# A fused attention and feed-forward block on one core: sums over eight chunks by a second transfer, both halves of the maxima on DVE, and rotary halves swapped by transfers

## The chip, the cores and the metric

The kernel runs on one core of a Trainium2 chip. The core has five engines with their own instruction streams: PE (TensorE, matrix products), DVE (VectorE), ACT (ScalarE), POOL (GpSimd) and SP (SyncE, which here only issues transfers). Each engine works through its own stream in order. Transfers (DMA) are issued from the queues of SP, ACT and POOL and share 16 DMA engines. The metric is the device time of one execution in microseconds, and its median over several runs.

## The reference

The input is x of shape (2, 2048, 512) in float32. The block computes a layer norm, attention with rotary positions and grouped keys (16 heads of width 32, 2 key groups), a residual, a second layer norm, and a product with a weight in fp8 values:

```python
x = x + attn(layernorm(x)); x = x + ffn(layernorm(x))
# attn, with h = layernorm(x)
q = (h @ wq + bq).reshape(b, s, 16, 32)
k = (h @ wk + bk).reshape(b, s, 2, 32);  v = (h @ wv + bv).reshape(b, s, 2, 32)
q = q * cos + rotate_half(q) * sin       # rotate_half: (-x2, x1) of the two halves of 16
k = k * cos + rotate_half(k) * sin
scores = einsum("bqhd,bkhd->bhqk", q * 32**-0.5, repeat(k)) * 32**-0.5
out = einsum("bhqk,bkhd->bqhd", softmax(scores), repeat(v)) @ wo + bo
# ffn: x and weight are scaled by max|.|/448, rounded to e4m3, multiplied, scaled back, bfloat16
```

## The kernel before

**Tiling.** The 4096 tokens are cut into 8 blocks (n) of 512. Four heads that share keys form a quad. A block has 4 quads, and each quad is treated in two halves of 256 queries: a *unit* (u), 64 in all. A unit goes over the 2048 keys of its batch element in 16 chunks (kc) of 128, four chunks to a *round* (r = 0 to 3).

**One unit.** The softmax needs the row maxima first. A generator, `scores_for_maxima` (L412 to L429), runs about one round ahead: for each of 64 combinations of 128 queries, a head and 512 keys PE writes a score tile `s` into one of two PSUM banks (L412), and DVE reduces it into `part` (L419). When a unit's tiles are through, DVE reduces `part` to `mx` (L426), ACT copies the rounded value to `mrow` (L427), and POOL writes the rest, mx minus the rounded value, beside it (L428). PE transposes `mrow` in the last round of the unit before (`mtp`, L439, in `gather_maxima`), and ACT copies the result to `mT` (L443).

In a round, `probabilities` lets PE subtract the maxima from T (L777, only for the first two chunks of a unit), add the scores of one chunk for four heads (L786), and ACT takes the exponential into a tile `p` of 128 x 1024 (L795). `columns` multiplies the four tiles `p` with the values (L746) and, into the other half of the same PSUM tile `avs`, tiles of sums with a matrix of ones (L757): the latter give the denominators.

**The sums.** To spare PE products with ones, tiles are first added. `add_pair` (L769) adds two tiles p on POOL into a tile `pa`. In rounds 0 to 2 this is done for both pairs, and a transfer on POOL's queue with an adding write (L836) adds the first `pa` to the second: `far_sum`, the sum over four chunks. Its product with ones follows one round later. In round 3 four tiles are multiplied: the far sum of round 2, the sum of the first pair, and the last two `p` as they are. A unit so has six products with ones: none in round 0, one each in rounds 1 and 2, four in round 3. Tiles `p` have five buffers, `pa` four.

**Filling work.** All else runs in gaps of this loop. Jobs are Python generators that yield the engine of their next step. `fill(kind)` takes a step from the first list (finishing, queue, beside) whose first job wants that engine: there are places for PE twice in a round (once in round 0) and for DVE twice at the end of a round. Jobs are: keys and values of the next batch element (`project_kv`), queries of the next block (`project_q`), the output product of the block before (`finish_block`), its second norm, and the feed-forward weight (`prepare_weight`, enqueued with block 4). The order is written out by hand inside `tc.manual_schedule()`; only the part behind the loop is ordered by the framework's scheduler.

**Rotary positions.** `rotated` (L274, L277) multiplies q or k on PE by a signed permutation matrix `rot_sb`, and DVE multiplies the result, in PSUM, by the sines into `u`. `rope` (L282, L283) lets POOL multiply q by the cosines and add u. `stack_queries` later splits q into a rounded part and a rest (L222, L223), writes both to DRAM and reads them back in the stacked layout `qst` (on SP's queue). Keys go the same way (`kS`, and `dkS`, differences to keys 256 earlier).

**Start and end.** Ahead of the loop, keys and values of the first batch element and the first two query tiles are projected; the jobs there use the same functions, with the flag `attending` off. Behind it, the fp8 stage goes over 16 half blocks: ACT scales (`v`, L872), DVE rounds with a helper tile `magic` (L210 to L216), PE transposes (L884), ACT copies (`xqT`, L886), PE multiplies (L889), ACT scales back (`y`, L893), DVE adds the residual (L894) and SP stores. `v` and `magic` take buffers of the tiles `p`.

Of the kernel before, what the change touches and what calls it, by code (L numbers as in the profile page):

```python
# [8 lines left out]
F32 = mybir.dt.float32  # L9
# [4 lines left out]
ALU = mybir.AluOpType  # L14
AX = mybir.AxisListType
# [12 lines left out]
def preln_attn_fp8_ffn_kernel(  # L28
# [60 lines left out]
    wide = ctx.enter_context(tc.tile_pool(name="wide", bufs=1))  # L89
    ppool = ctx.enter_context(tc.tile_pool(name="p", bufs=5))  # L90
    papool = ctx.enter_context(tc.tile_pool(name="pa", bufs=4))
    w2 = ctx.enter_context(tc.tile_pool(name="w2", bufs=6))
# [171 lines left out]
    def product(dst, lhs, rhs, chunks=DC):  # L264

        for c in range(chunks):
            yield ON_PE
            nc.tensor.matmul(dst, lhs(c), rhs(c), start=(c == 0), stop=(c == chunks - 1))  # L268

    def rotated(q, csb, name):  # L270

        yield ON_PE
        r = bank(f"r_{name}")
        nc.tensor.matmul(r, rot_sb, q, start=True, stop=True)  # L274
        yield ON_DVE
        u = t2(f"u_{name}")
        nc.vector.tensor_tensor(u, r, csb[:, 1, :], ALU.mult)  # L277
        return u
# [42 lines left out]
    def project_kv(n, xt, xnT, csb):  # L321
# [14 lines left out]
        nc.scalar.activation(kv, pk, AF.Identity, bias=bkv_sb)  # L336
        u = yield from rotated(kv, csb, f"k_{n}")
        yield ON_PE
        tv = bank(f"tv_{n}")
        for i in range(NT):  # L340
# [3 lines left out]
            tv.rearrange("p (i k) -> p i k", i=NT)[:, :, KD:],  # L344
        )
        rope(kx[:, BACK:], kv, u, KD, csb)
        cols = slice(blk * TB, (blk + 1) * TB)
        for what in ("kS", "dkS"):
# [9 lines left out]
            if b == 0:  # L358
                far = far.rearrange("(g d) h t -> d h g t", g=GROUPS)
                stack(  # L360
                    lambda rows: stacked[what][rows, :, cols],
                    [far[:, h, :, cols] for h in (0, 0, 1, 1)],
                )

    q_raw = {}

    def project_q(n, xnT, csb):
        q = wide.tile([P, QUADS, TB], F32, tag="q", name=f"q_{n}", bufs=2)
        for m in range(QUADS):
            pq = bank(f"pq_{n}_{m}")  # L370
            yield from product(
                pq, lambda c, m=m: wq_sb[:, c, m * P : (m + 1) * P], lambda c: xnT[:, c, :]
            )
            raw = t2(f"q_{n}_{m}")
            nc.scalar.activation(raw, pq, AF.Identity, bias=bq_sb[:, m : m + 1])
            u = yield from rotated(raw, csb, f"q_{n}_{m}")
            rope(q[:, m, :], raw, u, P, csb)
            q_raw[n, m] = q[:, m, :]

# [22 lines left out]
    def scores_for_maxima():  # L402

        for u, (k, half) in enumerate(units):
# [3 lines left out]
            for i, kb in order if u else sorted(order, key=lambda at: at[1]):  # L408
# [13 lines left out]
                if (i, kb) == (HT - 1, NKB - 1):  # L422
# [3 lines left out]
                    nc.vector.tensor_reduce(mx, part, AX.X, ALU.max)  # L426
                    nc.scalar.copy(mview[:, :, :, 0], mx)  # L427
                    nc.gpsimd.tensor_tensor(  # L428
                        mview[:, :, :, 1], mx, mview[:, :, :, 0].bitcast(F32), ALU.subtract  # L429
# [183 lines left out]
    class Job:  # L613


        def __init__(self, steps, kind=None):
            self.steps = steps
            self.kind = kind or next(steps)

        def step(self):  # L620
            self.kind = next(self.steps, None)

    queue = [Job(q0, ON_PE)]
    beside = []
    finishing = []
    attn_of = {}

    def work():

        queue[0].step()  # L630
        if queue[0].kind is None:
            queue.pop(0)

    def fill(kind, pieces=1):

        for _ in range(pieces):
            for jobs in (finishing, queue, beside):
                if jobs and jobs[0].kind in (kind, OTHER):
                    jobs[0].step()
                    if jobs[0].kind is None:  # L640
                        jobs.pop(0)
                    break

    x_res = {}
    x_taken, x_done = [], set()

# [24 lines left out]
    def enqueue(u):  # L671
        k, half = units[u]
        n, quad = quads[k]
        if half == 0 and quad == 0:
# [6 lines left out]
            if n + 1 < NBLK:  # L681
                take_x(f"q_{n + 1}")
                steps = later(project_q, n + 1, load_xnT(n + 1))
                queue.append(Job(ending(steps, f"q_{n + 1}")))
            if n == NB:
                take_x("w")
# [3 lines left out]

        first_use = (2, 0) if n <= NB else (1, 1) if n < NBLK - 1 else (0, 0)
        if n > 0 and (quad, half) == first_use:
            take_x(f"res_{n - 1}")
# [12 lines left out]
        if half == 0:  # L706
            if k + 1 < len(quads) and k + 1 not in qst:
                while quads[k + 1] not in q_raw:
                    work()
                stack_queries(k + 1)  # L710
            b = batch(k)
            if b + 1 < B and n == (b + 1) * NB - 1:
                if quad == 2:
                    fetch_keys("kS", b + 1, 0)
                    fetch_keys("dkS", b + 1, 0)
# [82 lines left out]
    with tc.manual_schedule():  # L798
        for _ in range(LEAD):
            next(scores)  # L800
        for u, (k, half) in enumerate(units):
# [9 lines left out]
            ]  # L811
            far_sum = None
            ending_soon = u >= len(units) - 2
            pieces = 2 if ending_soon else 1
            for r in range(ROUNDS):
                chunks = list(range(r * ROUND, (r + 1) * ROUND))
                last = r == ROUNDS - 1
                next(scores, None)
# [12 lines left out]
                if last:  # L831
                    sums = [far_sum, pair, *probs[2:]]
                else:
                    sums = [far_sum] if r > 0 else []
                    far_sum = add_pair(u, chunks[2], *probs[2:])
                    nc.gpsimd.dma_start(out=far_sum, in_=pair, accum_op=ALU.add)  # L836
                fill(ON_PE, pieces)
# [113 lines left out]
```

## Time and profile before

| what | value |
|---|---|
| median of 3 runs | 2548.15 us (2546.71 to 2550.91) |
| the profiled execution's own time | 2552.43 us |
| its span, first to last instruction | 2550.7 us |
| mean granted TensorE clock | 0.957 |
| busy: PE, DVE, ACT, POOL | 2308.2, 1703.0, 1209.6, 1531.0 us |
| last products of the attention loop | about 2431 us from the start |

The profile is of one execution. "Busy" is the time that an engine works on instructions; PE's is modelled and includes pipelining, so 90% is not 90% of its peak. A group of instructions is named by line, engine and operation, with the tile that it writes and those that it reads. The chain that ended last goes back from the last instruction, at each step to what released it. A list of waits puts the idle time of an engine down to the instruction that ended it: total in us, how often, the longest. The timeline gives start and duration in us, and in brackets the idle time before and what ended it; "x2" means that so many equal instructions are merged, which makes the duration that of the pair.

### The profile page before, as it was taken

Reading aid. Unit: us, or ns where it says so; the run is one execution under the profiler, and the core shown is the slowest. Engines: PE = TensorE matmul, PEld = TensorE weight load, DVE = VectorE, ACT = ScalarE, POOL = GpSimd, SP = SyncE. Lnnn points to the kernel's source line nnn. Section 1 sums busy time; section 2 is a strip of 40 time slices with the busy share of each in tenths; the row PEclk is TensorE's granted clock in tenths of the full one; section 3 lists DMA queues with packets and bytes.
Section 4 is the critical chain, followed back from the end, with each engine's and each line's share of the span. In section 5 each row is a group of like instructions: output and inputs, shape, how many; then the busy total and the mean of one; then the engine's idle time right before and its main releaser. Section 6 shows DMA issues by size and latency. Waiting matters only on the chain.

```text
span 2550.7 us, 41618 instructions
## 1 busy us (share of the span) xinstructions
PE 2308.2 (90%) x17094; PEld 1322.2 (52%) x17094; DVE 1703.0 (67%) x2706; ACT 1209.6 (47%) x1445; POOL 1531.0 (60%) x975
## 2 busy tenths in 40 slices
PE   5599999999999999988989989999989999989955
PEld 2355555555555555555555555555555555555522
DVE  3577657666677666865657786676666667667467
ACT  2155445554455444544445454445444544444545
POOL 4276756766667666665756756567656756656610
PEclk9599999999999999999999999999999999999957
DMA  7523333433234333443353433333343343343212
GB/s 227 153 50 87 79 100 83 100 92 99 60 89 91 85 100 83 109 102 64 92 121 71 92 83 67 87 72 75 67 100 91 75 116 67 72 111 100 50 42 99
DMA packets 85854, 229.77 MB, mean 90 GB/s; under 512 B 10656, under 2 KB 11296, under 8 KB 81824
## 3 DMA queue, kind: packets, MB, share of 16 engines
q0 software_dynamic: 27648, 100.68, 20.6%
q1 hardware_dynamic: 55600, 125.07, 16.3%
q8 instruction: 134, 2.20, 0.4%
q10 hardware_dynamic: 2416, 1.38, 0.2%
q14 instruction: 56, 0.46, 0.1%
HBM read 83.43 MB, written 42.99 MB: 50 GB/s over the span
## 4 chain that ended last, share of the span: by engine, by line
PE 59%; DVE 18%; POOL 7%; DMA 7%; issue 4%; ACT 4%; SPq 0%; POOLq 0%; ACTq 0%; DVEq 0%
PE s L412 15%; DVE part L419 13%; PE T L786 12%; PE avs L746 11%; PE avs L757 6%; DMA pa<-pa 6%; POOL pa L769 5%; PE po L268 4%; PE pq L268 4%; DVE both L729 2%; PE T L777 2%; ACT p L795 2%; PE py L889 2%; PE mtp L439 1%; PE r_q L274 1%
## 5 line engine op out<-in xcount | busy, mean ns | idle before, releaser
L419 DVE TENSOR_REDUCE part<-s 128x1 f32<-128x512 f32 x2048 | 1315.9, 685 | 724.8 <-PE s L412 710.9
L769 POOL TENSOR_TENSOR pa<-p,p 128x1024 f32<-128x1024 f32 x448 | 1064.6, 2381 | 566.8 <-ACT p L795 564.1
L795 ACT ACTIVATE p<-T 128x1024 f32<-128x1024 f32 x1024 | 1004.5, 1025 | 821.1 <-PE T L786 818.6
L412 PE MATMUL s<-kS,qst 128*128 128x512 f32 x2048 | 874.5, 480 | 62.3 <-DVE part L419 15.2
L786 PE MATMUL T<-qst,dkS 128*128 128x512 f32 x2048 | 682.4, 430 | 7.9 <-ACT p L795 7.9
L412 PEld LDWEIGHTS s<-kS,qst 128*128 128x128 f32 x2048 | 373.9, 192 | 500.2 <-DVE part L419 326.7
L746 PE MATMUL avs<-p,vX 128*32 128x256 f32 x8192 | 495.8, 382 | 0.0
L786 PEld LDWEIGHTS T<-qst,dkS 128*128 128x128 f32 x2048 | 374.4, 193 | 151.0 <-issue 49.9
L746 PEld LDWEIGHTS avs<-p,vX 128*32 128x32 f32 x8192 | 239.9, 110 | 216.2 <-issue 66.6
L836 POOL DMA_DIRECT2D pa<-pa x192 | 169.1, 881 | 60.7 <-POOL pa L769 57.8
L757 PE MATMUL avs<-pa,ones 128*32 128x256 f32 x2048 | 149.0, 386 | 46.7 <-DMA pa<-pa 46.7
L725 ACT COPY both<-avs 128x512 f32<-128x512 f32 x64 | 37.6, 587 | 237.2 <-PE avs L757 237.2
L268 PE MATMUL po<-wo_sb,attn 128*128 128x512 f32 x256 | 132.9, 604 | 3.4 <-POOL attn L730 3.4
L223 POOL TENSOR_TENSOR lo_q<-q,hi_q 128x512 fp32r<-128x512 f32 x32 | 41.4, 1292 | 145.9 <-ACT hi_q L222 145.8
L268 PE MATMUL pq<-xnT_q,wq_sb 128*128 128x512 f32 x224 | 118.7, 613 | 1.6 <-DVE u_q L277 1.6
L729 DVE RECIPROCAL both<-both 128x128 f32<-128x128 f32 x128 | 112.5, 920 | 5.8 <-ACT both L725 5.8
L757 PEld LDWEIGHTS avs<-pa,ones 128*32 128x32 f32 x2048 | 64.7, 110 | 96.8 <-DMA pa<-pa 56.1
L777 PEld LDWEIGHTS T<-mT,sel 128*128 128x128 f32 x512 | 79.0, 190 | 12.0 <-issue 0.4
L777 PE MATMUL T<-mT,sel 128*128 128x256 f32 x512 | 81.1, 281 | 0.0
L889 PE MATMUL py<-wT,xqT 128*128 128x512 bf16 x128 | 47.7, 513 | 29.5 <-ACT xqT L886 29.5
L730 POOL TENSOR_TENSOR attn<-both 128x256 f32<-128x256 f32 x64 | 65.6, 1024 | 7.7 <-DVE both L729 5.7
L757 PE MATMUL avs<-p,ones 128*32 128x256 f32 x1024 | 66.9, 379 | 0.0
(108 smaller groups left out, 1126.5 us busy)
## 6 DMA issues: line engine op xcount, KB each, us to landing
pa<-pa POOLq DMA_DIRECT2D x192, 512.0 KB, 4.6
qst<-q_far SPq DMA_DIRECT2D x128, 256.0 KB, 4.2
x_kv<-in_L_attn_x_dram SPq DMA_DIRECT2D x8, 1024.0 KB, 7.9
q_far<-hi_q SPq DMA_DIRECT2D x32, 256.0 KB, 2.0
q_far<-lo_q SPq DMA_DIRECT2D x32, 256.0 KB, 2.0
x_res<-in_L_attn_x_dram SPq DMA_DIRECT2D x8, 1024.0 KB, 7.5
out_dram<-v SPq DMA_DIRECT2D x16, 512.0 KB, 2.8
xnT_far<-xnT_kv SPq DMA_DIRECT2D x7, 1024.0 KB, 4.1
```

Of the source, the lines that this page charges most:

```text
L268: nc.tensor.matmul(dst, lhs(c), rhs(c), start=(c == 0), stop=(c == chunks - 1))
L412: nc.tensor.matmul(s, qst[k][:, j, at : at + P], stacked["kS"][:, group(k), kb * TB : (kb + 1) * TB], start=True, stop=True,)
L419: nc.vector.tensor_reduce(part[:, i, j, kb : kb + 1], s, AX.X, ALU.max)
L729: nc.vector.reciprocal(piece, piece)
L746: nc.tensor.matmul(avs[j * HD : (j + 1) * HD, 0, :], vX[batch(k)][:, kc, group(k), :], p[:, j, :], start=(kc == 0), stop=(kc == NTS - 1), ...
L757: nc.tensor.matmul(avs[j * HD : (j + 1) * HD, 1, :], ones, pa[:, j, :], start=False, stop=(chunks[-1] == NTS - 1 and i == len(sums) - 1), ...
L769: nc.gpsimd.tensor_tensor(pa, a, b, ALU.add)
L777: nc.tensor.matmul(T[:, j, :], sel[:, j, :], maxima[u], start=(j % 2 == 0), stop=True, skip_group_check=True,)
L786: nc.tensor.matmul(T[:, j : j + 2, :], stacked["dkS"][:, group(k), kc * P : (kc + 1) * P], qst[k][:, j : j + 2, half * HB : (half + 1) * H ...
L795: nc.scalar.activation(p, T, AF.Exp, scale=SCALE)
L836: nc.gpsimd.dma_start(out=far_sum, in_=pair, accum_op=ALU.add)
L889: nc.tensor.matmul(py, xqT[:, c, :], wT[:, c, :], start=(c == 0), stop=(c == DC - 1))
```

## The change

1. **Sums.** The far sums of rounds 0 to 2 are kept (`far_sums`) and none is multiplied before round 3. In round 2 a second adding transfer on POOL's queue adds the sum of round 0 to that of round 1, so that one tile covers eight chunks. Round 3 multiplies five tiles: the pair, two `p`, the sum over eight chunks, the far sum of round 2. Tiles `p` now have four buffers, `pa` five.
2. **Maxima.** The rounded copy into `mrow` and the subtraction both run on DVE.
3. **Rotary halves.** Inside the attention loop, `swapped` copies the halves of 16 rows crosswise into a new tile: eight transfers for a query tile, four for keys, on SP's queue. `rotate` then multiplies that tile by a sign (one value to a row) and the sines on DVE. The sign is the sum over a row of `rot_sb`, taken at the start of the kernel. This rotation and `rope` become jobs of their own (`turn`, `stack_keys`), put ahead in `beside`, and due two rounds later. Queries are written straight into the tile `q`. Ahead of the loop, `rotated` stays in use.
4. **Order.** `fill` looks at all jobs of `beside`, not only at the first, and passes over those that are not due. Loads of x for the residual are asked for when the queue is short, not at a fixed unit. `prepare_weight` is enqueued with block 6, not 4. Where queries or keys are not ready in time, `advance` steps both lists.

```diff
-    ppool = ctx.enter_context(tc.tile_pool(name="p", bufs=5))
-    papool = ctx.enter_context(tc.tile_pool(name="pa", bufs=4))
+    ppool = ctx.enter_context(tc.tile_pool(name="p", bufs=4))
+    papool = ctx.enter_context(tc.tile_pool(name="pa", bufs=5))
...
+    sign = const.tile([P, 1], F32, tag="sign", name="sign")
+    nc.vector.tensor_reduce(sign, rot_sb, AX.X, ALU.add)
+    nc.vector.tensor_scalar(sign, sign, -1.0, None, ALU.mult)
+
+    def swapped(q, rows, name):
+        t = t2(f"sw_{name}")
+        half = HD // 2
+        for at in range(0, rows, half):
+            to = at ^ half
+            nc.sync.dma_start(t[to : to + half, :], q[at : at + half, :])
+        return t
+
+    def rotate(t, csb, rows):
+        nc.vector.scalar_tensor_tensor(
+            t[:rows], t[:rows], sign[:rows], csb[:rows, 1, :], ALU.mult, ALU.mult
+        )
...
-        u = yield from rotated(kv, csb, f"k_{n}")
+        if attending[0]:
+            u = swapped(kv, KD, f"k_{n}")
+        else:
+            u = yield from rotated(kv, csb, f"k_{n}")
...
+        if attending[0]:
+            beside.insert(0, Job(stack_keys(n, kv, u, csb), due=step[0] + 2))
+        else:
+            yield from stack_keys(n, kv, u, csb)
+
+    def stack_keys(n, kv, u, csb):
+        b, blk = divmod(n, NB)
+        if attending[0]:
+            yield ON_DVE
+            rotate(u, csb, KD)
         rope(kx[:, BACK:], kv, u, KD, csb)
...
-            raw = t2(f"q_{n}_{m}")
+            raw = q[:, m, :]
             nc.scalar.activation(raw, pq, AF.Identity, bias=bq_sb[:, m : m + 1])
-            u = yield from rotated(raw, csb, f"q_{n}_{m}")
-            rope(q[:, m, :], raw, u, P, csb)
-            q_raw[n, m] = q[:, m, :]
+            if attending[0]:
+                u = swapped(raw, P, f"q_{n}_{m}")
+                beside.insert(0, Job(turn(n, m, raw, u, csb), due=step[0] + 2))
+            else:
+                u = yield from rotated(raw, csb, f"q_{n}_{m}")
+                rope(raw, raw, u, P, csb)
+                q_raw[n, m] = raw
+
+    def turn(n, m, raw, u, csb):
+        yield ON_DVE
+        rotate(u, csb, P)
+        rope(raw, raw, u, P, csb)
+        q_raw[n, m] = raw
...
-                    nc.scalar.copy(mview[:, :, :, 0], mx)
-                    nc.gpsimd.tensor_tensor(
+                    nc.vector.tensor_copy(mview[:, :, :, 0], mx)
+                    nc.vector.tensor_tensor(
                         mview[:, :, :, 1], mx, mview[:, :, :, 0].bitcast(F32), ALU.subtract
                     )
...
+            able = [
+                (jobs, job)
+                for jobs, some in ((finishing, 1), (queue, 1), (beside, len(beside)))
+                for job in jobs[:some]
+                if job.kind in (kind, OTHER) and job.due <= step[0]
+            ]
...
-            if n == NB:
+            if n == NBLK - 2:
                 take_x("w")
...
-        first_use = (2, 0) if n <= NB else (1, 1) if n < NBLK - 1 else (0, 0)
-        if n > 0 and (quad, half) == first_use:
+        soon = len(queue) <= 2 and u % (QUADS * HALVES) > 0 or n == NBLK - 1
+        if n > 0 and n - 1 not in x_asked and soon:
...
                 if last:
-                    sums = [far_sum, pair, *probs[2:]]
+                    sums = [pair, *probs[2:], *far_sums[1:]]
                 else:
-                    sums = [far_sum] if r > 0 else []
-                    far_sum = add_pair(u, chunks[2], *probs[2:])
-                    nc.gpsimd.dma_start(out=far_sum, in_=pair, accum_op=ALU.add)
+                    sums = []
+                    far_sums.append(add_pair(u, chunks[2], *probs[2:]))
+                    nc.gpsimd.dma_start(out=far_sums[r], in_=pair, accum_op=ALU.add)
+                if r == 2:
+                    nc.gpsimd.dma_start(out=far_sums[1], in_=far_sums[0], accum_op=ALU.add)
```

## The prediction

> **What bounds the kernel now.** First the page: which engine is full, and what the chain that ended last is made of.
>
> ```profile
> PE 2308.2 (90%) x17094; PEld 1322.2 (52%) x17094; DVE 1703.0 (67%) x2706; ACT 1209.6 (47%) x1445; POOL 1531.0 (60%) x975
> ...
> PE 59%; DVE 18%; POOL 7%; DMA 7%; issue 4%; ACT 4%; SPq 0%; POOLq 0%; ACTq 0%; DVEq 0%
> ```
>
> PE leads, but 18% of the chain is DVE and 14% POOL and DMA. So I look at one round (four chunks of keys) without filling work, in the chain in order of time:
>
> ```profile
> 1034.91 0.43 PE avs L757 x8
> 1035.35 0.66 PE s L412 x2
> 1036.00 0.93 PE T L786 x4
> 1036.93 0.72 PE s L412 x2
> 1037.65 0.73 PE T L786 x2
> 1038.38 0.24 PE s L412
> 1038.62 0.02 issue
> 1038.65 1.30 DVE part L419 x2
> ```
>
> One tile of sums costs PE 0.43 us (four products, two instructions each). PE then meets DVE: only two PSUM banks hold scores, and DVE must have reduced one before PE writes the next. Thus PE time taken out counts in full only where DVE isn't late. Last, who waits (the list of waits):
>
> ```profile
> PE avs L757 <- DMA pa<-pa: 46.7, 18, 6.9
> ...
> PE mtp L439 <- POOL mrow L428: 16.5, 10, 3.4
> ```
>
> The first line is PE waiting for an accumulating transfer.
>
> **Sums.** Sorting the 192 landings by round, nearly all of the 46.7 us (43 of them) belongs to the transfer of a unit's round 0, which lands after up to 14.2 us when it meets the transfers of stacked queries, and is wanted one round later. After the change no sum is wanted before round 3: **-47**. New there is the second transfer. Queue q0 used 20.6% of the 16 engines for 192 transfers, so one holds them 0.206 x 2550.7 / 192 = 2.74 us, and the second lands about that much after the first. In round 3 the first transfer now lands 3.4 us (median) before the end of the value products, 1.8 us in the worst tenth. The second's tile is used as fourth of five, 3 x 0.43 = 1.3 us later, but round 2 gets 0.43 shorter: 3.4 - 2.74 + 1.3 - 0.43 = 1.5 us to spare in the middle, -0.1 in the worst tenth: **+3** (0 to +6).
> Products with ones: now 1 tile in round 1, 1 in round 2, 4 in round 3; after it 0, 0 and 5. Each is 64 x 0.43 = 27.5 us. In round 1 I count 24 and in round 2 23, since in the rest DVE has no idle time before the next scores; round 3 pays 27.5, as DVE idles there 3 us: net **-20** (bounds -6 and -27.5).
> POOL issues 64 more transfers of 0.88 us (56 us) and loses 64 subtractions of 0.51 (33 us). It stays near 61% busy. The tiles of probabilities go from 5 buffers to 4: setting each exponential beside the POOL sum of the chunk four earlier, that sum had ended at least 1.5 us before in every case, so I count 0; a POOL later than that would stall ACT and then PE.
>
> **Maxima on DVE.** Today DVE hands the maxima (mx) to ACT and POOL, whose subtraction follows at 1010.70. Lines around one hand-over, in order of time:
>
> ```profile
> 1004.92 4.87 POOL L769 TENSOR_TENSOR pa<-p,p 128x1024 f32<-128x1024 f32 x2 [0.69 <-ACT p L795]
> ...
> 1008.66 0.19 DVE L426 TENSOR_REDUCE mx<-part 128x8 f32<-128x32 f32 x1
> ...
> 1010.30 2.68 DVE L419 TENSOR_REDUCE part<-s 128x1 f32<-128x512 f32 x4 [1.45 <-PE s L412]
> ```
>
> Gain: of the 16.5 us that PE waits for mrow about half, **-8**, as the longest three (3.3 us each) fall where ACT waits for POOL too. Cost: a copy (0.16, as COPY mean) and a subtraction (0.15, between the small two-input rows of 0.14 and 0.19). But the subtraction reads two SBUF tiles, and POOL's sum is then under way (here to 1009.79). What such an instruction does beside that sum, this trace shows once:
>
> ```profile
> 1481.63 4.71 POOL L769 TENSOR_TENSOR pa<-p,p 128x1024 f32<-128x1024 f32 x2 [0.42 <-ACT p L795]
> ...
> 1484.18 2.71 DVE L215 TENSOR_TENSOR w_scaled<-w_scaled,w_magic 128x512 f32<-128x512 f32 x1
> ```
>
> It took 2.71 us, up to 0.5 after POOL's end at 1486.34; the other three took 0.69. The Trainium skill's page "SBUF — State Buffer", section "Who interferes with whom", states the rule, and it speaks against this change: a DVE instruction with two SBUF inputs shares a port with a GpSimd instruction that reads SBUF, and the later one stands until the other is through. Blind use of the rule would charge a whole 2.38 us sum for each of 64, 152 us. By the rows only the rest of the running sum counts: 1.10 us on average at the 63 ends of mx + 0.16. Without the rule the pair costs 0.31 and hides altogether. What hides it is DVE's idle time before the next scores (1.45 above, 1.02 once the product with ones is gone). In two units of three the lateness is 0.31 + 1.10 - 1.02 = 0.4 or less (I take 0.3), in the third, where layer norms or other DVE work fill that gap, some 1.3: mean 0.62, x 63 = **+39**. Late in this way is the first reduction of round 3, then the transposes of the maxima, which need its bank; so I count it fully (bounds +5 and 63 x 1.41 = +89).
>
> **Rotary halves.** In the attention loop 30 tiles of queries and 4 of keys lose a product of 2 x 0.43 us: 34 x 0.86 = 29 if PE alone counted. But an unfilled round lasts 7.45 us (1027.83 to 1035.28), one with four such filling instructions 8.17 (1001.59 to 1009.76): 1.72 us of filling cost 0.72; over all rounds I fit 0.6 per us. So **-17** (bounds -12 and -29). Instead of u (from PSUM, 0.68), DVE multiplies two SBUF tiles by a sign: again behind POOL's sum, which at the ends of rounds 1 and 2 has 1.2 to 2.1 us left. The built order puts some 20 of 34 there, each about 0.6 us late: **+12** (0 to +25); the rest falls behind round 3, where DVE has 3 us.
> The swap: 30 x 8 + 4 x 4 = 256 transfers of 32 KB on SP. Four of the stacked queries' issues take 2.65 us, so eight take 5.3, and the last lands some 2 to 5 us later: under 11 us, beside the two rounds (15 us) that the job waits. SP's other work behind them (queries' halves, key loads) has a unit of 35 us. Counted 0. If cover fails, POOL's multiplication by cosines waits, and behind it all its sums.
> In-order waits of ACT for the keys' differences stay (31.2 us in hi_dkS before).
>
> **Start, end, moves.** The sum over rot_sb is DVE's first instruction. That load is issued at 3.07 and lands 6.7 us later, 9.75; DVE begins at 6.93 today: **+3**. At the end the fourth p buffer changes ACT's order:
>
> ```profile
> 2467.31 0.58 ACT L886 COPY xqT<-xtp 128x512 bf16<-128x512 bf16 x1
> 2467.77 1.53 ACT L872 ACTIVATE v<-y,plus,times 128x512 f32<-128x512 f32 x2
> 2469.93 0.69 ACT L893 ACTIVATE y<-py,y_scale 128x512 bf16<-128x512 f32 x1 [0.63 <-PE py L889]
> ```
>
> Now both v stand behind xqT while PE multiplies. In the built program one v stands between y and the next xqT, for which PE waits: 0.77 us x 15, **+11** (0 to +15). Residual loads and weight preparation move to other units; the two bursts in which a whole query product was pushed through at once go: **-3**.
>
> **Sum**: -47 + 3 - 20 - 8 + 39 - 17 + 12 + 3 + 11 - 3 = -27 us, against a profiled time of 2552.4 (span 2550.7), 4 us above the median 2548.15. From the median: **2521**.
>
> **Rivals.** (A) *DVE's new waits hide* (order shifts, POOL is ahead): maxima +5, rotation 0, removed products in full, -27.5 and -29, tail +5, and the other terms -47 + 3 - 8 + 3 - 3: -101, 2447. For it: DVE is 67% busy; against it: the short rows of 1.45 us. I hold 2440 to 2485 for it. (B) *DVE becomes the bound, slower*: place, the subtraction at the end of round 2 and the rotation at the ends of 1 and 2. If nothing hides (+89, +25), the sum is -27 + 50 + 13 = +36, 2584. It decides once the two terms exceed 51 + 27 = 78 us. For it: each wait recurs in every unit, and lateness in round 3 passes on to PE. (C) *The second transfer comes late* when it meets SP's traffic: a mean of 0.42 us over 64 units would eat the gain; with 1 us more, -27 + 64 = +37, 2585. Against: 1.5 us to spare, and stacked queries move in round 0. (D) *The swap changes nothing*: the rounds run at DVE's pace, the -17 is lost: -10, 2538; I keep it in the forecast's own range.
>
> **How the numbers follow.** A measurement here can tell some 0.2% (5 us) from no change. Forecast (with D), 2490 to 2552: 0.53; A 0.22; B 0.17; C 0.08. Faster by more than 0.2%: 0.44 of the forecast and A's 0.22, 0.66; within: 0.09 of the forecast and 0.01 of B, 0.10; slower: 0.24. The range takes most of A and B: 2455 to 2578; the likeliest alone 2490 to 2552.
>
> **What would show it.** No wait of PE for pa in rounds 1 and 2, a short one in some last rounds; the subtraction of maxima on DVE with a mean near 1.2 us, not 0.15; the rotation near 1.2 to 1.5 us where PE's product is gone; DVE's share of the chain above 18%; first statistics near 10 us; the tail from the last value product some 11 us longer. The prediction is wrong if those small DVE instructions run at 0.15 and 0.7, if POOL waits for swapped tiles, or if pa waits return in round 3.

## The result, and the profile after

The changed kernel takes 2557.48 us (median of 6 runs, 2549.36 to 2560.57); the kernel before, run beside it, 2549.43. The ratio is 1.0016, with a 95% interval of 0.9998 to 1.0035: no difference that can be told. The prediction was 2521, faster.

The profiled execution of the changed kernel took 2555.82 us, its span is 2554.0, 3.3 more than before. The page, with the busy times and the chain by engine:

```profile
PE 2292.0 (90%) x16514; PEld 1301.2 (51%) x16514; DVE 1824.7 (71%) x2836; ACT 1196.8 (47%) x1381; POOL 1573.9 (62%) x975
...
PE 54%; DVE 29%; POOL 5%; issue 3%; DMA 3%; ACT 3%; SPq 1%; DVEq 0%; POOLq 0%; ACTq 0%
```

PE executes 580 matmuls fewer, but is busy only 16 us less. DVE is on the chain with 29% where it was 18%; transfers have gone from 7% to 3%. The list of waits says the same by name (engine, line, what it waited for: us in total, times, longest). PEld is PE's loading of weights. First a line of the kernel before, then lines of the changed one:

```profile
PE s L412 <- DVE part L419: 15.2, 17, 2.6
```

```profile
PEld s L457 <- DVE part L464: 417.3, 933, 6.2
...
PE s L457 <- DVE part L464: 79.2, 63, 5.8
...
PE avs L806 <- DMA pa<-pa: 1.2, 2, 0.8
```

PE's 46.7 us of waits for an adding transfer are down to 1.2. PE's wait for DVE before a score product was 15.2 us (17 times) and is 79.2 (63 times in 64 units). The chain in order of time (start, duration, what) shows where in a unit:

```profile
1045.46 1.30 DVE part L464 x2
1046.76 0.02 issue
1046.78 0.20 DVE mx L471
1046.98 0.02 issue
1047.00 1.36 DVE mrow L472
1048.36 0.02 issue
1048.39 0.17 DVE mrow L473
1048.56 0.59 DVE amax L533
1049.15 0.45 DVE xn L524
1049.61 1.90 DVE part L464 x3
1051.51 0.04 issue
1051.55 0.44 PE mtp L484 x2
```

This is the end of round 2. From the last reduction of one unit to the first of round 3 everything is DVE: the maxima, their copy, their subtraction, two filling steps. PE works in between (on scores from 1047.73), but the chain comes back to it only at 1051.55, since its third score product had to wait for DVE. The copy alone takes 1.36 us. The view of the tile `mrow` gives both instructions (duration in ns: shortest, median, longest):

```profile
L472 DVE CAST mrow<-mx x64: 175/1332/2127, 114.6 to 2380.2; 128x8 fp32r<-128x8 f32 x64
L473 DVE TENSOR_TENSOR mrow<-mx,mrow x64: 174/176/2312, 114.8 to 2381.2; 128x8 fp32r<-128x8 f32 x64
```

The two groups that the change added elsewhere, as the lines by form list them (busy us, mean ns, idle before):

```profile
L888 POOL DMA_DIRECT2D pa<-pa x64 | 75.7, 1183 | 11.7 <-DMA pa<-pa 10.2 <-issue 1.5
...
L286 DVE SCALAR_TENSOR_TENSOR sw_q<-sw_q,sign,cs 128x512 f32<-128x512 f32 x30 | 42.8, 1432 | 0.7 <-DMA sw_q<-q 0.7
```

The second transfer's issue is recorded with 1.18 us, not the 0.89 of the others, but its record begins 0.30 us (median) before the end of the one ahead of it: from end to end it takes POOL 0.89 us, as they do. DVE waits 0.7 us in all for swapped tiles.

To see where time went I cut both executions where the last product into `avs` of each round begins: start (to that of the first round), loop (to that of the last round), tail. The loop gained 10.6 us (2298.3 to 2287.7), the start 1.6 (133.2 to 131.6), and the tail lost 15.6 (119.1 to 134.7). Inside the loop round 0 gained 16 us, round 1 gained 68, round 2 gained 1, and round 3 lost 74.

The same cut shows a thing that the prediction leaves out, and that the experiments below name only as a rival for the tail: the TensorE clock that was granted. The view by stretches gives it as the third number from the end (before it the busy times of PE, PEld, DVE, ACT, POOL), loop and tail of the kernel before and then of the changed one:

```profile
133.20:2431.50 2298.30, 2165.11 (x16598) 1255.42 (x16591) 1558.08 (x2476) 1122.84 (x1305) 1485.13 (x923) 0.98 0.37 86
2431.50:2550.00 118.50, 64.70 (x271) 26.31 (x263) 88.22 (x118) 60.37 (x97) 1.43 (x2) 0.67 0.18 71
131.60:2419.30 2287.70, 2141.42 (x16019) 1233.88 (x16011) 1676.60 (x2602) 1109.94 (x1242) 1528.14 (x924) 0.97 0.47 105
2419.30:2554.00 134.70, 75.62 (x271) 28.96 (x263) 90.78 (x118) 60.74 (x97) 1.43 (x2) 0.58 0.16 63
```

In these traces the granted share is either 1 or 0.5. The loop spent 81.9 us at half clock before and 116.0 after, the tail 78.7 and 114.4. One product into T follows the next after 232 ns at full and 427 at half clock (medians, changed kernel), so a stretch at half clock can cost PE up to half its length.

### The profile page after: what moved, and what is told of

It is laid out like the page before. It is cut to its first block, busy times and chain, and to the rows that moved or that the text cites. A ratio compares the mean times of both kernels' runs of the same rounds, so it can differ in the third digit from the quotient of the medians.

```text
span 2554.0 us, 41075 instructions
## 1 busy us (share of the span) xinstructions
PE 2292.0 (90%) x16514; PEld 1301.2 (51%) x16514; DVE 1824.7 (71%) x2836; ACT 1196.8 (47%) x1381; POOL 1573.9 (62%) x975
## 3 DMA queue, kind: packets, MB, share of 16 engines
q0 software_dynamic: 36864, 134.23, 27.7%
q1 hardware_dynamic: 63792, 133.47, 17.7%
## 4 chain that ended last, share of the span: by engine, by line
PE 54%; DVE 29%; POOL 5%; issue 3%; DMA 3%; ACT 3%; SPq 1%; DVEq 0%; POOLq 0%; ACTq 0%
DVE part L464 19%; PE s L457 14%; PE T L835 11%; PE avs L795 9%; PE avs L806 5%; PE po L268 4%; PE pq L268 3%; POOL pa L818 3%; DVE both L778 2%; PE T L826 2%; PE py L941 2%; DVE mrow L472 2%; ACT p L844 1%; PE mtp L484 1%; DVE sw_q L286 1%
## 5 line engine op out<-in xcount | busy, mean ns | idle before, releaser
L818 POOL TENSOR_TENSOR pa<-p,p 128x1024 f32<-128x1024 f32 x448 | 1078.1, 2411 | 497.1 <-ACT p L844 486.2
L457 PE MATMUL s<-kS,qst 128*128 128x512 f32 x2048 | 882.8, 483 | 137.8 <-DVE part L464 79.2
L886 POOL DMA_DIRECT2D pa<-pa x192 | 170.1, 886 | 60.9 <-POOL pa L818 58.3
L806 PE MATMUL avs<-pa,ones 128*32 128x256 f32 x1536 | 106.3, 379 | 3.1 <-POOL pa L818 2.0
L941 PE MATMUL py<-wT,xqT 128*128 128x512 bf16 x128 | 56.6, 593 | 35.3 <-ACT xqT L938 35.3
L888 POOL DMA_DIRECT2D pa<-pa x64 | 75.7, 1183 | 11.7 <-DMA pa<-pa 10.2
L472 DVE CAST mrow<-mx 128x8 fp32r<-128x8 f32 x64 | 76.3, 1192 | 2.2
```

The costliest lines, as they stand in the source:

```text
L457: nc.tensor.matmul(s, qst[k][:, j, at : at + P], stacked["kS"][:, group(k), kb * TB : (kb + 1) * TB], start=True, stop=True,)
L472: nc.vector.tensor_copy(mview[:, :, :, 0], mx)
L806: nc.tensor.matmul(avs[j * HD : (j + 1) * HD, 1, :], ones, pa[:, j, :], start=False, stop=(chunks[-1] == NTS - 1 and i == len(sums) - 1), ...
L818: nc.gpsimd.tensor_tensor(pa, a, b, ALU.add)
L886: nc.gpsimd.dma_start(out=far_sums[r], in_=pair, accum_op=ALU.add)
```

## Experiments

Theory at first: the maxima on DVE, behind POOL's sum, take back the gain of the sums. Rivals: the second transfer (late, or its place in POOL's queue), the fifth `p` buffer, products with ones that PE never had to pay for. The kernel before is measured anew beside each group of runs (medians 2550.8 to 2554.7 us, single executions 2542 to 2567), so ratios are compared. "Changed" is the kernel after the change.

### The maxima moved back

```diff
 # changed kernel
-nc.vector.tensor_copy(mview[:, :, :, 0], mx)
-nc.vector.tensor_tensor(
+nc.scalar.copy(mview[:, :, :, 0], mx)
+nc.gpsimd.tensor_tensor(
```

> The changed kernel with the maxima's copy back on ACT and the subtraction back on POOL; all else stays. Theory (the two small DVE instructions stand behind POOL's sum, and that lateness goes through to PE in round 3): round 3 falls from a mean of 11.86 us by 0.6 to 0.75, the run from 2557 to 2510 to 2520. Rival (round 3 is long because of its five products with ones and the second transfer): no more than 10 us move, 2547 to 2560.

Measured: 2550.61 us, ratio 0.9988 [0.9976, 0.9999]. The gain is the rival's (the loop takes 2288.5 us, against 2287.7 in the changed kernel), but the theory isn't refuted by it: PE's wait for POOL's `mrow` is now 55.0 us (47 times), against 16.5 (10) before the change. One wait was exchanged for another. A second form, in which DVE writes the rounded value by a second reduction and POOL subtracts:

```diff
-nc.vector.tensor_copy(mview[:, :, :, 0], mx)
-nc.vector.tensor_tensor(
+nc.vector.tensor_reduce(mview[:, :, :, 0], part, AX.X, ALU.max)
+nc.gpsimd.tensor_tensor(
```

> The changed kernel with the rounded maxima written by a second reduction over part on DVE (one SBUF input, 0.19 us) in place of the copy, and the subtraction on POOL. Theory (the port): neither DVE instruction waits for POOL, 2510 to 2520, round 3 as with the maxima back on ACT and POOL. Rival (not the port, but that DVE does one more thing and hands over later): still above 2540.

2551.3 us, 0.9986 [0.9977, 0.9996]: the same, by the same wait on POOL (52.3 us, 47 times), and again the rival's range. So neither run shows what the copy costs the kernel. The second does show what the copy itself was waiting for: the reduction in its place took 176 to 180 ns in all 64 uses.

### The maxima alone, in the kernel before

```diff
 # kernel before
-nc.scalar.copy(mview[:, :, :, 0], mx)
-nc.gpsimd.tensor_tensor(
+nc.vector.tensor_copy(mview[:, :, :, 0], mx)
+nc.vector.tensor_tensor(
```

> The kernel before with only the maxima's copy and subtraction moved to DVE. Theory: +30 to +45 us from DVE's lateness, less some 8 us of PE's wait for POOL: 2570 to 2590, and it shows in round 3, whose mean rises from 10.7 by 0.4 to 0.6 us. Rival (the move itself is harmless): 2540, 8 us less than before.

2580.87 us, ratio 1.0095 [1.0061, 1.013]; the loop is 24.0 us longer (2322.3), 27 of it in round 3. Alone, this part makes the kernel slower by about 1%, within the theory's range.

### The rotary halves back on PE, and the sums alone

```diff
 # changed kernel: also inside the loop
-u = swapped(raw, P, f"q_{n}_{m}")
-beside.insert(0, Job(turn(n, m, raw, u, csb), due=step[0] + 2))
+u = yield from rotated(raw, csb, f"q_{n}_{m}")
+rope(raw, raw, u, P, csb)
# and so for the keys; no sign
```

> The changed kernel with the rotary halves turned by PE and rot_sb again (no swaps, no sign, no jobs of their own for it); sums, maxima and order of filling as in the change. Prediction's own terms: -17 of PE against +12 of DVE and +3 at the start, so nearly no move: 2555 to 2565. Rival 1 (PE's 29 us count in full): 2575 or more. Rival 2 (the swap costs more than it gives): under 2550.

2576.1 us, ratio 1.0079 [1.0051, 1.0106], loop 17.5 us longer than the changed kernel's: the rival's number. The swap is worth something here.

```diff
 # kernel before: p 4 and pa 5 buffers, and
-sums = [far_sum, pair, *probs[2:]]
+sums = [pair, *probs[2:], *far_sums[1:]]
-sums = [far_sum] if r > 0 else []
+sums = []
+if r == 2:
+    nc.gpsimd.dma_start(out=far_sums[1], in_=far_sums[0], accum_op=ALU.add)
```

> The kernel before with the sums over eight chunks alone (and with them four buffers for p and five for pa); maxima on ACT and POOL, rotation by PE, order of filling as before. By the prediction's terms (-47 +3 -20 in the loop, +11 at the end): 53 us faster than before. Theory formed since (the second transfer's issue stands in POOL's queue ahead of the subtraction of the maxima and of the layer norms' powers): PE's wait for mrow grows from 16 to about 55 us and some last rounds get 5 to 6 us longer, so that only 0 to 20 us are left.

2562.97 us, ratio 1.0044 [1.0031, 1.0057]. The loop gains only 5 us and the tail loses 17. PE's waits for `pa` are down to 2.9 us, and again PE waits for POOL's `mrow`, 71.7 us (56 times), more than the 55 that the theory had, and of its 0 to 20 us nothing is left. The prediction's -64 for the sums in the loop (-47 + 3 - 20) did not appear even without the other parts.

### The second transfer issued one round later

```diff
 # changed kernel: not in round 2, but
 pair = add_pair(u, chunks[0], *probs)
+if last:
+    nc.gpsimd.dma_start(out=far_sums[1], in_=far_sums[0], accum_op=ALU.add)
...
-sums = [pair, *probs[2:], *far_sums[1:]]
+sums = [pair, *probs[2:], far_sums[2], far_sums[1]]
```

> The changed kernel with the second transfer issued in round 3, behind the sum of that round's first pair, and its tile multiplied last. Theory (POOL's queue): the four last rounds that are 5.5 us too long (units 37, 45, 55, 59, where a layer norm's power and then DVE stand behind two transfer issues) become normal, PE waits at most 20 us in all for the late tile: 2530 to 2545. Rival (the transfer now lands too late): a wait of PE of 1 us or more in each last round, over 2600. Rival (POOL's queue does not matter): 2550 to 2560.

2616.05 us, ratio 1.0247 [1.0209, 1.0285]. Its list of waits:

```profile
PEld avs L806 <- DMA pa<-pa: 55.1, 35, 4.8
...
PE avs L806 <- DMA pa<-pa: 39.0, 26, 4.3
```

Issued in round 3 the transfer lands too late, as the first rival had it. The same with the maxima on ACT and POOL:

> As a_late2, and the maxima's copy on ACT and subtraction on POOL. Theory (the maxima on POOL cost so much only since they stood behind the second transfer): PE's wait for mrow falls from 55 back to about 17 us: 2490 to 2515. Rival (the wait for mrow is due to POOL's sums, not to the transfer's issue): 2530 to 2550, mrow waits of 40 us or more.

2598.1 us, ratio 1.0166 [1.0122, 1.0209]. PE's wait for POOL's `mrow` fell to 12.4 us (10 times), so it does come from the issue in round 2; but the wait for `pa` is 64.7 us, and the theory's 2490 to 2515 us is missed. With the maxima on POOL neither of the two places that were tried is free.

### The fifth p buffer

The fp8 stage's helper tile is put where the rotary tables were, which are dead by then:

```diff
-magic = ppool.tile([P, 2, D], F32, tag="p", name=f"magic_{n}_{half}")
+magic = cs.tile([P, 2, D], F32, tag="cs", name=f"magic_{n}_{half}")
```

> The changed kernel with the helper tile of the fp8 stage in the free buffer of the rotary tables, so that v alone has the four p buffers. Theory (the lost fifth buffer makes the end longer): what follows the last product with ones falls from 134.7 us to 120 to 128 us, the run by 7 to 15; the loop stays within 3 us. Rival (the end is longer for the lower granted clock there): no change.

2537.49 us, ratio 0.9942 [0.9921, 0.9963]; the tail goes from 134.7 to 117.6 us. The two orders of ACT, first in the changed kernel:

```profile
2460.50 0.69 ACT L945 ACTIVATE y<-py,y_scale 128x512 bf16<-128x512 f32 x1 [1.98 <-PE py L941]
2461.09 0.80 ACT L924 ACTIVATE v<-y,plus,times 128x512 f32<-128x512 f32 x1
2461.79 0.57 ACT L938 COPY xqT<-xtp 128x512 bf16<-128x512 bf16 x1
```

and with the tile moved:

```profile
2460.91 0.69 ACT L945 ACTIVATE y<-py,y_scale 128x512 bf16<-128x512 f32 x1 [1.98 <-PE py L941]
2461.49 0.58 ACT L938 COPY xqT<-xtp 128x512 bf16<-128x512 bf16 x1
2461.96 1.53 ACT L924 ACTIVATE v<-y,plus,times 128x512 f32<-128x512 f32 x2
```

In the changed kernel one `v` stands between `y` and `xqT`, which PE is waiting for; with the buffer free both stand behind it. PE's wait for `xqT` is 29.5 us before the change, 35.3 in the changed kernel and 31.5 here; the tail's time at half clock is 78.7, 114.4 and 70.2 us. All later runs have this edit.

### No second transfer

Instead each far sum is multiplied two rounds after it was formed: none in round 1, round 0's in round 2, the rest in round 3. That takes the waits away and leaves six products in a unit.

```diff
-sums = []
+sums = [far_sums[0]] if r == 2 else []
-if r == 2:
-    nc.gpsimd.dma_start(out=far_sums[1], in_=far_sums[0], accum_op=ALU.add)
```

In the kernel before (nothing else of the change but the buffers, and the tile `magic` moved):

> The kernel before with no second transfer: the sum of round 0 goes into PE's products only in round 2, that of round 1 only in round 3, so that each has two rounds to land; six products with ones for a half block as before (none in round 1, one in round 2, five in round 3). Maxima on ACT and POOL, rotation by PE, p 4 and pa 5 buffers, and the fp8 stage's magic tile in the free rotary-table buffer. First terms: the waits for pa alone are worth 43 to 47 us, and products moved between rounds cost nothing in sum: 2495 to 2510, a ratio of 0.982, with PE's wait for POOL's mrow back near before's 16.5 us. Rival (what the run with all of the sums' change showed): a wait taken away comes back as a wait for scores or maxima, so a gain of 5 to 15 us: 2535 to 2545.

2501.01 us, ratio 0.9804 [0.979, 0.9819], the theory's range, though PE's wait for POOL's `mrow` is 25.6 us (18 times) and not back at 16.5. In the changed kernel:

> The changed kernel with the magic tile in the free rotary-table buffer (2537.5 so, at a ratio of 0.994) and with no second transfer: round 0's sum is multiplied in round 2, round 1's and 2's in round 3, one product with ones more for a half block (64 times some 0.37 us, 24 us of PE). Theory that the second transfer's issue on POOL (64 times 1.18 us) is what round 3 lost: that round falls from a mean of 11.9 to about 11.3 us in spite of its five products against five, round 2 gains a product but no more than 0.35 us, in sum 2515 to 2530. Rival, the issue is hidden beside DVE's waits anyway: the product counts in full and the time is 2550 to 2565.

2537.98 us, ratio 0.9944 [0.9926, 0.9961], the same as with the transfer (0.9942), and neither the theory's range nor the rival's. And with the maxima back on ACT and POOL:

> The same, and the maxima's copy back on ACT and their subtraction on POOL, where no second transfer's issue stands ahead of it now. Theory: PE's wait for POOL's mrow falls from 55.0 us (the changed kernel with the maxima moved back) to about the 16.5 of before and DVE is free of 1.63 us in each half block: 2495 to 2510. Rival: DVE's share of the maxima was hidden and POOL's share is no cheaper, so no more than 10 us from the run beside it: 2510 to 2530 if that run is 2515 to 2530, and no faster than the changed kernel with the magic tile moved.

2500.39 us, ratio 0.9798 [0.9784, 0.9813]. Now, with nothing in POOL's way, the maxima's place is worth 37.6 us, where moving them back in the changed kernel had brought 0.3%. PE's wait before scores (34.4 us, 27 times) and that for POOL (8.3 us) in its list of waits:

```profile
PE s L457 <- DVE part L464: 34.4, 27, 6.6
...
PE mtp L484 <- POOL mrow L473: 8.3, 9, 2.1
```

### The transfer and the product taken apart

The run without the transfer neither gained nor lost; two effects could have cancelled: the product more (24 us in round 2) and the transfer away (29 us in round 3: from 758.9 to 730.0). Two kernels keep all six products and only put the transfer back, in full or as 16 of the 1024 elements of a partition (round 0's sum, or a part of it, is then counted twice):

```diff
 # the changed kernel with no second transfer
+if r == 2:
+    nc.gpsimd.dma_start(out=far_sums[1], in_=far_sums[0], accum_op=ALU.add)
# or:  out=far_sums[1][:, 0, :16], in_=far_sums[0][:, 0, :16]
```

> The run with no second transfer (2538 us, ratio 0.9944), with the second transfer put back where the change has it, and all six products with ones kept, so round 0's sum is counted twice and the output is not the reference's. Theory that the transfer's issue and what stands behind it cost round 3 some 29 us: ratio 1.004 to 1.008, 2562 to 2573 against a before of 2552, round 3 from a mean of 11.41 to about 11.85 us. Rival, the transfer costs nothing and the two earlier runs differ for another reason (the product taken out of round 2 was hidden): ratio 0.993 to 0.997, round 3 within 0.1 us of 11.41.

> The same with a second transfer of 16 elements a partition in place of 1024 (8 KB and not 512 KB), in the same place of POOL's queue; all six products kept, so a small part of round 0's sum is counted twice. If POOL's queue is what costs (the issue's time and what stands behind it), this is near the run with the full transfer, a ratio of 1.002 to 1.008, as far as the issue takes as long (some 0.9 to 1.2 us). If the 512 KB on the transfer engines or their arrival at PE cost, it is near the run without one, 0.994 to 0.997.

Ratios 0.9931 [0.9904, 0.9958] and 0.993 [0.9906, 0.9953], 2535.19 and 2536.08 us: my theory of 29 us fell. With the maxima on DVE the transfer costs nothing that these runs can tell, and the issue takes as long for 8 KB as for 512 KB. So the product that it saves was worth nothing that they can tell either (0.9931 with it, 0.9942 without). The last pair completes the table where the maxima are on ACT and POOL: the transfer alone, and the product alone (round 0's sum left out).

```diff
 # the 2500 us kernel
+if r == 2:
+    nc.gpsimd.dma_start(out=far_sums[1], in_=far_sums[0], accum_op=ALU.add)
# or, without it:
-sums = [far_sums[0]] if r == 2 else []
+sums = []
```

> No product saved, maxima on ACT and POOL (2500 us, ratio 0.9798 without a second transfer), and the second transfer put back in round 2, so that round 0's sum is counted twice and the output is not the reference's. Theory: its issue stands ahead of the maxima's subtraction in POOL's queue and PE waits for it: PE's wait at mtp for POOL's mrow rises from under 20 us to 40 to 60 us, ratio 0.990 to 0.995. Rival: it costs no more than beside the maxima on DVE (3 us), ratio 0.980 to 0.983.

> Maxima on ACT and POOL, no second transfer, and the sum of round 0 left out of the products, so that the sums miss four of sixteen chunks and the output is not the reference's: one product with ones less for a half block than the 2500 us run (64 times some 0.37 us). Theory that DVE with the maxima on it was what hid the product: freed of them, PE's product counts, 15 to 24 us, ratio 0.970 to 0.974. Rival, the product is hidden here too (POOL or the scores' reduction set round 3's start): ratio 0.977 to 0.981.

The transfer: 2537.91 us, ratio 0.9938 [0.992, 0.9957], 37 us dearer, the theory's ratio, with a wait a little under its 40 us. (Its profile is of the longest of 12 executions, 2548.35 us.) In the timeline, POOL's queue at one hand-over:

```profile
1015.87 0.88 POOL L886 DMA_DIRECT2D pa<-pa  x1 [0.30 <-POOL pa L818]
...
1016.46 1.19 POOL L888 DMA_DIRECT2D pa<-pa  x1
...
1017.02 0.87 POOL L473 TENSOR_TENSOR mrow<-mx,mrow 128x8 fp32r<-128x8 f32 x1
...
1017.94 0.44 PE L484 MATMUL mtp<-ident,mrow 128*128 128x128 f32 x2 [0.52 <-POOL mrow L473]
```

The maxima were ready at 1013.72. Both issues run ahead of the subtraction, and PE waits for it. Over 64 units the mean time from the end of `mx` to the end of the subtraction rises from 2.97 to 4.04 us, and PE's wait there from 8.3 to 37.1 us.

The product alone: 2494.37 us, ratio 0.9775 [0.9757, 0.9792], 6 us, where the theory had 15 to 24. The rival is right: most of the saving is hidden here too, with DVE freed of the maxima.

| maxima on | second transfer, product saved | no transfer, product kept | transfer, product kept | no transfer, product left out |
|---|---|---|---|---|
| DVE | 0.9942 | 0.9944 | 0.9931 | not run |
| ACT and POOL | 0.9988 (with the long tail) | 0.9798 | 0.9938 | 0.9775 |

## Why the prediction was wrong

The runs form a path from the kernel before to the changed one, a step at a time. Each row is one profiled execution, us. Rows whose loop has the same work differ by up to 2 us in it, and by up to 8 in start and tail; but whole executions of one kernel spread over 15 us and more in some groups, so the two smallest steps (3.3 and 2.9) can't be told from nothing, and medians are named below where they say otherwise. The steps are worth this in this order, with the maxima moved before the transfer is added; the table above shows that another order gives other values. The last two columns are of round 3: PE's idle time before score products, summed from the gaps in the trace, and the time at half clock.

| kernel | loop | round 0 | round 1 | round 2 | round 3 | tail | idle | half clock |
|---|---|---|---|---|---|---|---|---|
| before | 2298.3 | 527.6 | 556.6 | 529.6 | 684.5 | 119.1 | 13.1 | 34.1 |
| sums two rounds later, buffers, magic tile moved | 2254.1 | 525.7 | 483.3 | 520.0 | 725.1 | 111.7 | 14.2 | 51.2 |
| + swap by transfers, job order | 2248.8 | 511.6 | 488.3 | 550.7 | 698.2 | 115.6 | 26.4 | 27.3 |
| + maxima on DVE | 2282.9 | 511.5 | 488.5 | 552.9 | 730.0 | 116.6 | 57.3 | 47.8 |
| + second transfer | 2286.2 | 511.5 | 488.4 | 554.2 | 732.1 | 110.5 | 54.7 | 54.6 |
| + product of round 2 taken out | 2289.1 | 511.6 | 488.4 | 527.0 | 762.1 | 117.6 | 76.1 | 78.5 |
| + magic tile in the p buffers (changed) | 2287.7 | 511.6 | 488.6 | 528.7 | 758.9 | 134.7 | 73.5 | 79.0 |

Against the prediction's own terms:

| step | predicted | measured |
|---|---|---|
| waits for pa, product out of round 1, one more in round 3 | -47 - 24 + 27.5 = -43.5 | -44.2 |
| rotation (-17 + 12), moves and bursts (-3) | -8 | -5.3 |
| maxima on DVE (+39, PE's wait for POOL -8) | +31 | +34.1 |
| second transfer late | +3 | +3.3 |
| product out of round 2 | -23 | +2.9 |
| tail | +11 | +15.6 |
| start | +3 | -1.6 |
| rest of the loop | 0 | -1.4 |

**The step that failed** is one term in "Products with ones": "In round 1 I count 24 and in round 2 23, since in the rest DVE has no idle time before the next scores". Round 1's counts. Round 2's does not, +2.9 us where -23 was forecast, and these 26 us are nearly all of the distance between the forecast sum, -27, and the measured span, +3.3. The row where the product is taken out shows round 2 shorter by 27 us and round 3 longer by 30. PE arrives 0.43 us earlier in round 3 and stands there until DVE has reduced a score tile: before the third score product of that round it now stands in 45 units, 69.1 us in all, where it stood in 31 units and 48.4 us with the product kept. All of PE's idle time in round 3 is up by 17.7 us. The other 12 of the 30 us agree with the clock: round 3 spends 24 us more at half clock, which costs up to 12. The prediction has no term for the granted clock. Half clock goes with PE's idle time: in the changed kernel's loop there are 25 stretches of it, and in the 3.4 us ahead of each PE had been idle for 1.3 us or more (2.1 in the mean, against 0.22 ahead of an average moment). That the idle time brings the lower clock is likely from this, but no run here holds one and changes the other.

With the maxima off DVE it goes the same way: round 2 -25, round 3 +19 (717.6 against 698.2), a gain of 6 us in sum by the medians. Round 3 begins behind the end of one unit's maxima, with filling work around it; what PE wins just ahead of it is lost in it. The prediction had the test for this in its first part ("PE time taken out counts in full only where DVE isn't late") but took it at one place only, DVE's idle time before its next reduction, and not where PE then stands, before the third score product.

The maxima belong to the same place. The prediction charged them with the shorter gap too (1.45 to 1.02 us): 0.3 us in two of three units, some 13 of its 39 us. The runs show the maxima costing 34 us (37.6 by the medians) with the gap still whole, where its own working leaves some 18 (39 - 13 - 8). So that its size of 31 came out right is luck. The place as a whole, product and maxima, was forecast with +8 and cost +37. In round 3, which takes 31.8 of the 34, PE's idle time is up by 15.7 us and half-clock time by 20.5, which costs up to 10. How the 34 us divide between the wait for POOL and the two instructions' plain time was not isolated, as each kernel that moves one of them to POOL puts it behind the issue there. A slip of the prediction's sums changes nothing here: the terms of rival A add up to -98.5, not -101.

**What was right.** The waits for `pa` and the moved products, in sum to 1 us; by rounds, round 1 gained 73.3 where 71 was forecast. The rest is in part luck: round 3 lost 40.6, not 27.5, and round 2, for which nothing was forecast, gained 9.6. The half-clock time can account for most of both (round 3 from 34.1 to 51.2 us, round 2 from 34.6 to 3.4). The second transfer's arrival, 1.2 us of waits where 3 were charged. DVE's share of the chain rose. The rotation's duration is 1.43 us (1.2 to 1.5 was named).

**The tail** became longer by the change of ACT's order that was forecast: moving one tile takes it back. But of the 15.6 us only 5.8 are more waiting for `xqT`, where 11 was charged; PE's same 271 products there keep it busy 10.9 us longer (75.62 against 64.70), with 36 us more at half clock.

**The copy, not the subtraction.** For the pair of maxima instructions 1.41 us was charged and 1.63 measured (1192 + 441 ns), though it is the copy that stands. The prediction weighed the Trainium skill's page "SBUF — State Buffer", section "Who interferes with whom", for the subtraction with its two SBUF inputs; the section also names copies and casts, which may take the port pair that DVE shares with GpSimd. I had charged the copy at 0.16 us. The trace agrees with the page: in 55 of 64 uses the copy began during a POOL sum and ended 0.03 to 0.04 us after it. Once it has waited, that sum is over, and the subtraction takes 0.176 us in the median (0.441 in the mean: 8 of 64 began during another sum and took 2.2 to 2.3 us).

**The swap** and the job order gave 5 us of the loop on the path above, where 8 was forecast, but the medians of the two kernels differ by 0.6 us (2501.01 and 2500.39), so this can't be told from nothing. Undone in the changed kernel, the swap is worth 17.5 us of loop. The two cases differ in maxima and sums beside it; I have not found which of these makes it dearer.

**The start** could not be judged: DVE does wait until 9.9 us for `rot_sb`, as predicted, but the last of the first round's products begins between 130.8 and 139.1 us in kernels whose start is the same code, in the changed kernel at 131.6 and before at 133.2. A shift of 3 us isn't to be seen in that.

**Why the first experiments misled.** "POOL stays near 61% busy" was true (62%), and a share says nothing about order. The second transfer costs nothing that can be told while the maxima are on DVE and 37 us while their subtraction is on POOL. So the sums done alone (5 us of the loop) and the maxima moved back (0.3%) both looked worthless. The maxima on DVE and the second transfer can be judged only together. Neither is needed: sums used two rounds later, in a kernel that otherwise is the one before, take 2501 us, and with the swap beside it 2500.

## What to carry to other kernels

A wait for a late transfer could be cured here by using the result later, at no cost in instructions; look for that before adding a transfer that needs a place in a queue. Compare the granted clock of the stages too: here PE's idle time was not all that it lost. Time taken from one engine counts only if the next thing that it meets isn't late: check the very place behind the saving, where the engine would next have to wait. When undoing a part changes nothing, read the waits of that run before believing it: here a wait on DVE had been exchanged for one on POOL, and only a kernel free of both showed what each was worth.

## What the hardware showed that I had not expected

- A copy of 128x8 elements with one SBUF input took 175 ns or up to 2127 (median 1332) on DVE beside POOL's sums of two 128x1024 tiles: in 55 of 64 uses it ended 29 to 39 ns after the sum that was running when it began. A reduction to the same 128x8 elements, in the copy's place, took 176 to 180 ns each time. In the kernel before, the same copy on ACT took a mean of 207 ns.
- An adding transfer's issue holds POOL 0.89 us, for 8 KB as well as for 512 KB. Directly behind another one its record is longer (1185 and 1183 ns), but the two records overlap by 0.30 us. So do those of a subtraction and the issue ahead of it: the subtraction reads 0.52 us behind one issue and 0.84 behind two (means), and ends 0.25 us after the last issue in both cases.
- 64 adding transfers of 512 KB more raised their queue's share of the transfer engines from 20.6% to 27.7% and, with the maxima on DVE, moved the time by nothing that these runs can tell.
- PE's granted clock dropped to half for 3.4 to 10.2 us at a time, in all 82 us of the loop before (16 times) and 116 in the changed kernel (25 times), though PE was busy 90% of the span in both. Each time PE had been idle for 1.3 us or more of the 3.4 us ahead.
